# Layer 1 of a two-layer graph network: parts of 40, 40, 36 and 12 graphs instead of 40, 40, 40 and 8

## The chip, the cores and the metric

The kernel runs on one core of a Trainium2 chip. The metric is device time in microseconds (us) of one execution; lower is better. Times of "before" are the median of three runs. A profiled execution gives the trace; it has a time of its own, which stands beside its span below.

## The reference

There are 128 graphs of 128 nodes with 256 features each, all in float32. Two layers follow each other, both with a normalisation in front and a residual sum behind:

```
h = relu(layernorm(x));  x = x + L0(h, adj)
h = relu(layernorm(x));  x = x + L1(h, adj)

L0: conv 1x1 and conv of 17 taps with batch norms, a message product with
    A = exp(-dist) * adj, then a GRU cell over [conv, message] and h
L1: for each of 5 groups g of nodes (25, 9, 7, 6 and 6 nodes out of the first 25):
        A   = D^-1/2 (adj_g + I) D^-1/2
        hid = relu(A @ (h_g @ W1[g]) + b1[g])          # 256 -> 512
        out = relu(A @ (hid @ W2[g]) + b2[g])          # 512 -> 256
        fused[nodes of g] += softmax(fusion_w)[g] * out
```

Layer 1 touches only the first 25 nodes of a graph. The outputs are `out0` (the other 103 nodes, finished after layer 0) and `out1` (the 25 nodes, finished after layer 1).

## The kernel before

The graphs go in blocks of four (`BB`), so there are 32 blocks (`NBLK`). A front stage computes the convolution in the frequency domain and ends at about 470 us. Then comes the main loop over the blocks `i`: `gates(i, step, nxt)` issues the matmuls of the GRU cell (L666), and calls `step` between them. `step` hands out one piece of other work at a time. Turn by turn it takes either a piece of `first`, which is `beside_gates(i + 1)` and prepares the next block, or, on every second turn or when `first` is used up, a piece of layer 1. All these pieces are Python generators; each `yield` ends a piece. In the last block (`i == NBLK - 1`) a turn of layer 1 takes two pieces.

`beside_gates(i)` also contains `back(i - 2)`, the end of block `i - 2`: it adds the result to `xt`, copies the first 25 nodes to `xl` (L817), stores `out0` (L818), turns and normalises the 25 nodes (L830 to L839), multiplies them with the adjacency block `ae` (L843) and leaves the product in `ab` (L848). For the first three parts `xl` and `ab` go to scratch memory in DRAM (`xf`, L820, and `xa`, L853). For the last part (`LAST`) they stay on the chip, in `kept["f"]` and `kept["ax"]`.

Layer 1 works on parts of graphs, `PARTS`. `layer1(k)` is started when all blocks of part `k` have passed their gates: it is appended to `layer1s` after the gates of the block that follows the part, so part 2 of "before" comes after block 30's gates. It loads `f` (L959), waits for some turns, and goes over chunks. A chunk is a list of packs of at most 512 columns (a pack is a run of graphs of one group with at most 128 columns). For each group in a chunk, `first` multiplies with W1 (L934: 8 matmuls, as wide as the group's columns in the chunk), and ACT (L941) and DVE (L939) write `hh` in turn. Then each pack is multiplied with W2 (L994: 4 matmuls of 256 columns), ACT scales the result into `s2` (L997), and one pack later `last` multiplies it with the pack's adjacency tile `nt` (L913), ACT makes `og` (L916), and DVE adds it to `f` (L922). At the end `f` is stored to `out1` (L1008).

Three helpers issue loads while this goes on. `ax_load(n + 1)` loads the next chunk's `ax` (L905, tag "ax", two buffers). `prepare(j)` loads adjacency and degree tiles of pack `j + 5` (L864, L867) and lets DVE turn those of pack `j + 2` into `nt` (L871, L872). `weights1` and `weights2` load the weights of a later group (L881, each 512 KB) once the buffer of an earlier one is free: there are two buffers for W1 and three for W2. All these loads and stores are issued from one queue, SP's, in its order. A float32 matmul of the program appears as two records on PE in the trace.

Two buffers matter for the change. In "before" the last part's `kept["f"]` has the tag "f8", and `kept["ax"]` takes one of the two buffers of the tag "ax", for good, from the moment block 30's `back` runs.

After the loop the last block's end is written out by hand:

```python
end = back(NBLK - 1, *back_loads(NBLK - 1))
next(end)
for steps in (2, 1):
    next(end)
    for _ in range(steps):
        step()
for _ in end:
    pass
while layer1s:
    step()
for _ in layer1(LAST):
    pass
```

The program's instructions pass a scheduler that may move them on an engine; the order named in the text is the one that it made.

Of the kernel before, what the change touches and what calls it, by code (L numbers as in the profile page):

```python
# [8 lines left out]
F32 = mybir.dt.float32  # L9
# [4 lines left out]
P = 128  # L14
# [3 lines left out]
BB = 4  # L18
# [3 lines left out]
WCH = 32  # L22
STEP = 3
NR = LW - P
PARTS = [40, 40, 40, 8]
NN = 25
HID = 512
MW = 130
# [20 lines left out]
GW = GOFF[-1]  # L49
# [15 lines left out]

PACKS = [(k, p) for k, size in enumerate(PARTS) for c in _chunks(size) for p in c]

# [4 lines left out]
STOP = object()  # L72
# [3 lines left out]
def gnn_kernel(ctx: ExitStack, tc: tile.TileContext, io, out0: bass.AP, out1: bass.AP):  # L76
    nc = tc.nc
    x, adjT = io["x"], io["adjT"]
    NBLK, N, _, D = x.shape
    B, C = NBLK * BB, D // P  # L80
# [387 lines left out]
    l1 = ctx.enter_context(tc.tile_pool(name="l1", bufs=2, reuse_waits="tile"))  # L468
# [280 lines left out]
    def degrees(a, b, cs):  # L749
# [30 lines left out]
        for c0, c1, d in ((F0, K0, dvf), (K0, E0, dvk)):  # L780
# [5 lines left out]

    xa = [dram.tile([P, C, size * GW // BB], F32, tag=f"xa{k}", name=f"xa{k}") for k, size in enumerate(PARTS)]
    xf = [dram.tile([P, C, size, NN], F32, tag=f"xf{k}", name=f"xf{k}") for k, size in enumerate(PARTS)]
    first_of = [sum(PARTS[:k]) for k in range(len(PARTS) + 1)]
    where = [next((k, i * BB - first_of[k]) for k in range(len(PARTS)) if i * BB < first_of[k + 1])  # L790
             for i in range(NBLK)]
    LAST = len(PARTS) - 1
    kept = {}
# [9 lines left out]
    def back(i, ae, dc):  # L803

        xt, o = xts.pop(i), outs.pop(i)
        for c in range(C):
            nc.vector.tensor_add(xt[:, c, :], xt[:, c, :], o[:, c, :])
        xv = xt.rearrange("p c (b n) -> p c b n", b=BB)
        k, b0 = where[i]
        if k == LAST:  # L810
            if not kept:
                kept["f"] = l1.tile([P, C, PARTS[k], NN], F32, tag="f8", name="f8", bufs=2)
                kept["ax"] = l1.tile([P, C, 512], F32, tag="ax", name="ax", bufs=2)
            xl = kept["f"][:, :, b0:b0 + BB, :]
        else:
            xl = wk.tile([P, C, BB, NN], F32, tag="xl", name="xl", bufs=2)
        nc.vector.tensor_copy(xl, xv[:, :, :, :NN])  # L817
        nc.sync.dma_start(out0[i], xv[:, :, :, NN:])  # L818
        if k != LAST:
            nc.sync.dma_start(xf[k][:, :, b0:b0 + BB, :], xl)  # L820
        yield

        nc.vector.tensor_add(ae[:n4], ae[:n4], ie[:n4])
        for g in range(len(GROUPS)):
            av = ae[:n4, GOFF[g]:GOFF[g + 1]]
            nc.vector.tensor_scalar(av, av, dinv[:n4, E0 + 5 * i + g:E0 + 5 * i + g + 1], None, op0=ALU.mult)
        yield
        ps = bank()
        for c in range(C):
            nc.tensor.transpose(ps[:n4, c * P:(c + 1) * P], xl[:, c].rearrange("p b m -> p (b m)"), ident)  # L830
        st = l1.tile([P, 6], F32, tag="st", name="st", bufs=2)
        mv = l1.tile([P, 4], F32, tag="mv1", name="mv1", bufs=2)
        nc.vector.bn_stats(st[:n4], ps[:n4, :D])
        nc.vector.bn_aggr(mv[:n4, 0:2], st[:n4])
        nc.vector.tensor_scalar(mv[:n4, 2:3], mv[:n4, 1:2], EPS, None, op0=ALU.add)
        nc.gpsimd.tensor_tensor(mv[:n4, 3:4], mv[:n4, 2:3], mhalf[:n4, 0:1], op=ALU.pow)
        hn = l1.tile([P, D], F32, tag="hn", name="hn", bufs=1)
        nc.vector.tensor_scalar(hn[:n4], ps[:n4, :D], mv[:n4, 0:1], 0.0, op0=ALU.subtract, op1=ALU.max)
        nc.scalar.mul(hn[:n4], hn[:n4], mv[:n4, 3:4])  # L839
        yield  # L840
        ps = bank()
        for c in range(C):
            nc.tensor.matmul(ps[:, c * GW:(c + 1) * GW], hn[:n4, c * P:(c + 1) * P], ae[:n4], start=True, stop=True)  # L843
        if k == LAST:
            ab = kept["ax"][:, :, b0 // BB * GW:(b0 // BB + 1) * GW]
        else:
            ab = l1.tile([P, C, GW], F32, tag="ab", name="ab", bufs=1)
        nc.vector.tensor_tensor(ab, ps[:, :C * GW].rearrange("p (c m) -> p c m", c=C),  # L848
                                dc[:, None, :].to_broadcast([P, C, GW]), op=ALU.mult)
        if k != LAST:  # L850
            for g, (s, _) in enumerate(GROUPS):
                at = PARTS[k] * GOFF[g] // BB + b0 * s
                nc.sync.dma_start(xa[k][:, :, at:at + BB * s], ab[:, :, GOFF[g]:GOFF[g + 1]])  # L853
        yield
# [35 lines left out]
    def layer1(k):  # L890
        size, k5 = PARTS[k], len(GROUPS) * k
# [4 lines left out]
        for chunk in chunks:  # L896
            g, b0, _ = chunk[0]
# [56 lines left out]
        if k == LAST:  # L954
            f = kept["f"]
        else:
            tag = "f" if size > 8 else f"f{size}"
            f = l1.tile([P, C, size if size <= 8 else max(PARTS), NN], F32, tag=tag, name=tag, bufs=1 if size > 8 else 2)
            nc.sync.dma_start(f[:, :, :size, :], xf[k])  # L959
            yield  # L960
            for _ in range(8 if size > 8 else 2):
                yield
        for n, chunk in enumerate(chunks):
            ax_load(n + 1)
            hh = l1.tile([P, HID // P, 512], F32, tag="hh", name="hh", bufs=1)
            segs, done, at = [], {}, 0
            for g, b0, nb in chunk:
                m = nb * GROUPS[g][0]
                if not segs or segs[-1][0] != g:
                    segs.append((g, at, []))  # L970
                segs[-1][2].append((b0, nb, at, j))
                at += m
                done[g] = at if ends[g] == j else None
                j += 1
            bounds = [a for _, a, _ in segs] + [at]
            for t in range(len(segs) + 1):
                if t < len(segs):
                    g, m0, _ = segs[t]
                    m1 = bounds[t + 1]
                    if k == LAST:  # L980
                        xv = kept["ax"][:, :, :PARTS[k] // BB * GW].rearrange("p c (b m) -> p c b m", m=GW)
                        xv = xv[:, :, :, GOFF[g]:GOFF[g + 1]]
                    else:
                        xv = axs[n][:, :, m0:m1]
                    yield from first(g, m0, m1, xv)
                if t:
                    g, _, packs = segs[t - 1]
                    for b0, nb, at, jj in packs:
                        prepare(jj)
                        n1 = nb * GROUPS[g][0]  # L990
                        nt = ready.pop(jj)
                        ps = bank()
                        for q in range(HID // P):
                            nc.tensor.matmul(ps[:n1, :D], hh[:, q, at:at + n1], w2s[k5 + g][:, q, :],  # L994
                                             start=q == 0, stop=q == HID // P - 1)
                        s2 = l1.tile([P, D], F32, tag="s2", name="s2", bufs=3)
                        nc.scalar.mul(s2[:n1, :], ps[:n1, :D], dinv[:n1, K0 + jj:K0 + jj + 1])  # L997
                        if late:
                            last(*late.pop(0))
                        late.append((g, b0, nb, s2, nt))  # L1000
                        if jj == ends[g]:
                            weights2(k5 + g + 4)
                        yield
# [75 lines left out]
    layer1s = []  # L1079
    for i in range(NBLK):  # L1080
        first = beside_gates(i + 1) if i else second
        turn = [0]

        def step():

            next(degs, None)
            turn[0] += 1
            if (turn[0] % 2 if i else turn[0] % 3) and next(first, STOP) is not STOP:
                return
            for _ in range(2 if i == NBLK - 1 else 1):  # L1090
                while layer1s and next(layer1s[0], STOP) is STOP:
                    layer1s.pop(0)

        if i + 2 < NBLK:
            load_h(i + 2)
            load_y(i + 2)
        xts[i] = wk.tile([P, C, T], F32, tag="xt", name="xt", bufs=2)
        nc.sync.dma_start(xts[i], io["xT"][i])

        def nxt():  # L1100
            for _ in first:
                pass
            if i + 1 < NBLK:
                gate_inputs(i + 1, (0, 1))
            if i + 2 < NBLK:
                gate_inputs(i + 2, (2,))

        gates(i, step, nxt, None if i else sums_ahead)
        if (i + 2) * BB == PARTS[0]:
            for q in (-5, -4, -3):  # L1110
                prepare(q)
        for k in range(len(PARTS)):
            if i * BB == first_of[k + 1]:
                layer1s.append(layer1(k))

    end = back(NBLK - 1, *back_loads(NBLK - 1))
    next(end)
    for steps in (2, 1):
        next(end)
        for _ in range(steps):  # L1120
            step()
# [129 lines left out]
```

## Time and profile before

| what | value |
|---|---|
| median of 3 runs | 1843.83 us (1843.5 to 1846.31) |
| the profiled execution, its own time | 1844.07 us |
| its span in the trace | 1842.3 us |
| PE busy | 1825.6 us, 99% |
| DVE, ACT, POOL busy | 72%, 40%, 35% |
| W1 matmuls of layer 1 (L934) | 416 records |
| W2 matmuls of layer 1 (L994) | 480 records |
| last gate matmul of block 31 starts | 1792.40 us |
| last matmul of all starts (group of 8) | 1836.31 us |

PE is the matmul engine (TensorE), PEld its weight loads, DVE the vector engine, ACT the scalar engine, POOL GpSimd, SP the queue that issues transfers. L666 is line 666 of the kernel. A row such as "L994 PE MATMUL bank<-w,hh" names line, engine, operation, and output and inputs by the program's names. An arrow in square brackets gives the idle time in front of an instruction and what ended it. In the answers by windows each engine has its busy time in the stretch and its number of instructions; then come the clock granted to PE, the share of the DMA engines' time, and GB/s. Ends of matmuls are modelled, so spacings from start to start say more than durations.

### The profile page before, as it was taken

The numbers are of one execution on the slowest core, as the hardware profiler recorded it, in microseconds if no ns is written. First come the engines' busy times: TensorE is split into PE (matmuls) and PEld (weight loads), VectorE is DVE, ScalarE is ACT, GpSimd is POOL, SyncE is SP. The second block draws the span as 40 slices with busy tenths as digits, with TensorE's granted clock in tenths as the row PEclk, the third lists the DMA queues.
The fourth block names the chain that finished last, engine by engine and source line by source line (L and its number), as shares of the span: only waits on it lengthen the run. The fifth ranks groups of instructions, "written<-read, shape, count | busy, mean of one in ns | idle before, by whom it ended". The sixth has DMA issues, their size and how long they took to land.

```text
span 1842.3 us, 31240 instructions
## 1 busy us (share of the span) xinstructions
PE 1825.6 (99%) x10982; PEld 1591.2 (86%) x10982; DVE 1326.4 (72%) x3296; ACT 731.7 (40%) x1619; POOL 646.7 (35%) x803
## 2 busy tenths in 40 slices
PE   8999999999999999999999999999999999999998
PEld 6888888888888888888888888888888888888787
DVE  6888865555887878887665778778756677888543
ACT  4666641112434343334334333433343343333334
POOL 1111125675444443544221344435312243544200
PEclk9999999999999999999999999999999999999999
DMA  7888888996633333334324433333333433232125
GB/s 292 315 316 316 304 286 303 354 316 236 179 74 79 79 90 81 91 73 113 75 92 119 114 93 75 76 87 111 78 91 91 127 89 95 74 78 70 36 91 159
DMA packets 219420, 267.96 MB, mean 145 GB/s; under 512 B 106211, under 2 KB 182968, under 8 KB 217216
## 3 DMA queue, kind: packets, MB, share of 16 engines
q1 hardware_dynamic: 214079, 248.04, 44.9%
q10 hardware_dynamic: 5184, 17.93, 2.4%
q8 instruction: 87, 1.43, 0.3%
q14 instruction: 70, 0.57, 0.1%
HBM read 169.24 MB, written 96.67 MB: 144 GB/s over the span
## 4 chain that ended last, share of the span: by engine, by line
PE 94%; DVE 2%; DMA 2%; POOL 1%; SPq 0%; issue 0%; ACT 0%; ACTq 0%; DVEq 0%; POOLq 0%
PE bank L666 45%; PE bank L335 6%; PE bank L239 6%; PE bank L994 5%; PE bank L934 5%; PE bank L567 5%; PE bank L255 3%; PE bank L330 3%; PE bank L546 3%; PE bank L617 3%; PE bank L175 2%; PE bank L225 1%; PE bank L913 1%; PE bank L843 1%; DMA nt<-in_adjN_dram 1%; PE bank L528 1%
## 5 line engine op out<-in xcount | busy, mean ns | idle before, releaser
L666 PE MATMUL bank<-t,sw 128*128 128x256 f32 x1152 | 291.3, 380 | 0.6 <-DVE nn L681 0.3
L679 POOL TENSOR_TENSOR u<-u,m 128x256 f32<-128x256 f32 x128 | 95.4, 745 | 475.4 <-ACT m L677 404.5
L666 PEld LDWEIGHTS bank<-t,sw 128*128 128x128 f32 x1152 | 215.0, 190 | 32.3 <-issue 2.1
L666 PE MATMUL bank<-t,wih 128*128 128x256 f32 x768 | 200.3, 383 | 0.0
L666 PEld LDWEIGHTS bank<-t,wih 128*128 128x128 f32 x768 | 143.1, 190 | 28.8 <-DVE o L706 7.3
L239 PE MATMUL bank<-wc,ht 128*128 128x256 f32 x512 | 126.5, 392 | 0.0
L327 POOL TENSOR_TENSOR vs<-v 128x256 f32<-128x256 f32 x134 | 98.3, 759 | 71.3 <-DMA v<-vd 42.0
L994 PE MATMUL bank<-w,hh 128*125 128x256 f32 (+9 forms) x480 | 114.2, 380 | 1.0 <-DVE hh L939 1.0
L666 PE MATMUL bank<-xc,wih 128*128 128x256 f32 x384 | 114.6, 380 | 0.1
L666 PE MATMUL bank<-t,whh 128*128 128x256 f32 x384 | 114.5, 380 | 0.0
L666 PE MATMUL bank<-xn,wih 128*128 128x256 f32 x384 | 114.2, 379 | 0.0
L590 ACT ACTIVATE msg<-msg 128x512 f32<-128x512 f32 x64 | 36.8, 621 | 190.5 <-DVE msg L586 190.5
L666 PE MATMUL bank<-ht,whh 128*128 128x256 f32 x384 | 109.8, 380 | 0.0
L239 PEld LDWEIGHTS bank<-wc,ht 128*128 128x128 f32 x512 | 94.5, 194 | 15.0 <-issue 0.2
L934 PE MATMUL bank<-ax,w 128*128 128x500 f32 (+8 forms) x416 | 107.0, 396 | 0.0
L550 ACT ACTIVATE xc<-xc,bn 128x512 f32<-128x512 f32 x64 | 46.2, 722 | 151.1 <-DVE xc L549 151.0
L209 POOL TENSOR_TENSOR rs<-ve,mhalf 128x4 f32<-128x4 f32 x32 | 32.3, 1009 | 209.0 <-DVE ve L207 201.3
L994 PEld LDWEIGHTS bank<-w,hh 128*125 128x125 f32 (+9 forms) x480 | 84.1, 178 | 20.1 <-DVE hh L939 2.6
L184 ACT COPY sp<-bank 128x408 f32<-128x408 f32 (+1 forms) x160 | 66.8, 509 | 71.9 <-PE bank L175 68.9
L324 DVE SCALAR_TENSOR_TENSOR s<-X 128x256 f32<-128x256 f32 x67 | 46.7, 698 | 64.4 <-PE bank L335 64.4
L934 PEld LDWEIGHTS bank<-ax,w 128*128 128x128 f32 x416 | 69.8, 190 | 19.4 <-issue 12.3
L684 DVE TENSOR_TENSOR u<-bank,u 128x256 f32<-128x256 f32 x128 | 53.5, 418 | 42.9 <-PE bank L666 42.4
(206 smaller groups left out, 4363.8 us busy)
## 6 DMA issues: line engine op xcount, KB each, us to landing
vd<-sp SPq DMA_DIRECT2D x16, 2176.0 KB
v<-vd SPq DMA_DIRECT2D x34, 1024.0 KB
w<-in_w_dram SPq DMA_DIRECT2D x40, 512.0 KB
ln<-in_x_dram SPq DMA_DIRECT2D x32, 512.0 KB
htd<-ht SPq DMA_DIRECT2D x32, 512.0 KB
yd<-ys ACTq DMA_DIRECT2D x32, 512.0 KB
ht<-htd SPq DMA_DIRECT2D x32, 512.0 KB
ym<-yd SPq DMA_DIRECT2D x32, 512.0 KB
```

Source lines behind the costliest of these rows:

```text
L184: nc.scalar.copy(dst, s)
L239: nc.tensor.matmul(pv[:, bb, :], ht[:, c, b * N:(b + 1) * N], wc1[:, c, :], start=c == 0, stop=c == C - 1)
L255: nc.tensor.matmul(ps[:, bb * LW:(bb + 1) * LW], h1[:, 2 * h + bb, c * P:(c + 1) * P], fd, start=True, stop=True)
L327: nc.gpsimd.tensor_tensor(vs[:, c], vr[c], vi[c], op=ALU.add)
L330: nc.tensor.matmul(p1[:, :D], a[:, c], vs[:, c], start=c == 0, stop=c == C - 1)
L335: nc.tensor.matmul(ps[:, k * D:(k + 1) * D], u[:, c], w[c], start=c == 0, stop=c == C - 1)
L546: nc.tensor.matmul(ps[:, b * N:(b + 1) * N], ym[:, 2 * h + b, o * P:(o + 1) * P], idm, start=False, stop=b == 1)
L567: nc.tensor.matmul(ps[:, b, :], d[:, b * N:(b + 1) * N], w, start=True, stop=True)
L666: nc.tensor.matmul(ps, w, d, start=n == 0, stop=n == len(pairs) - 1)
L679: nc.gpsimd.tensor_tensor(got["u4"], got["u2"], got["m5"], op=ALU.add)
L934: nc.tensor.matmul(pv[:, q - q0, :], w1s[k5 + g][:, c, q * P:(q + 1) * P], xv[:, c], start=c == 0, stop=c == C - 1)
L994: nc.tensor.matmul(ps[:n1, :D], hh[:, q, at:at + n1], w2s[k5 + g][:, q, :], start=q == 0, stop=q == HID // P - 1)
```

## The change

The parts are 40, 40, 36 and 12 graphs. The last part so holds three blocks (29, 30 and 31) and the third nine, and `layer1(2)` is started after block 29's gates. The last part gets buffers of its own, "fl" for its features and "axl" for its products, each just as large as needed; the second "ax" buffer stays with `ax_load`. A turn of layer 1 takes one piece in every block. Beside the end of the last block six and two pieces are taken instead of two and one. The branches for a third part of eight graphs or fewer are gone. Lines after L954 move by one or two.

```diff
-PARTS = [40, 40, 40, 8]
+PARTS = [40, 40, 36, 12]
...
             if not kept:
-                kept["f"] = l1.tile([P, C, PARTS[k], NN], F32, tag="f8", name="f8", bufs=2)
-                kept["ax"] = l1.tile([P, C, 512], F32, tag="ax", name="ax", bufs=2)
+                kept["f"] = l1.tile([P, C, PARTS[k], NN], F32, tag="fl", name="fl", bufs=1)
+                kept["ax"] = l1.tile([P, C, PARTS[k] // BB * GW], F32, tag="axl", name="axl", bufs=1)
...
-            tag = "f" if size > 8 else f"f{size}"
-            f = l1.tile([P, C, size if size <= 8 else max(PARTS), NN], F32, tag=tag, name=tag, bufs=1 if size > 8 else 2)
+            f = l1.tile([P, C, max(PARTS), NN], F32, tag="f", name="f", bufs=1)
             nc.sync.dma_start(f[:, :, :size, :], xf[k])
             yield
-            for _ in range(8 if size > 8 else 2):
+            for _ in range(8):
                 yield
...
-                        xv = kept["ax"][:, :, :PARTS[k] // BB * GW].rearrange("p c (b m) -> p c b m", m=GW)
+                        xv = kept["ax"].rearrange("p c (b m) -> p c b m", m=GW)
...
-            for _ in range(2 if i == NBLK - 1 else 1):
-                while layer1s and next(layer1s[0], STOP) is STOP:
-                    layer1s.pop(0)
+            while layer1s and next(layer1s[0], STOP) is STOP:
+                layer1s.pop(0)
...
-    for steps in (2, 1):
+    for steps in (6, 2):
         next(end)
         for _ in range(steps):
             step()
```

The chunks of the parts follow from their sizes. Written as groups with their columns, a chunk in each bracket:

| part | chunks (columns of each group) |
|---|---|
| 40 graphs | (g0 500) (g0 500) (g1 360, g2 91) (g2 189, g3 240) (g4 240): 18 packs |
| 8 graphs | (g0 200, g1 72, g2 56, g3 48, g4 48): 6 packs |
| 36 graphs | (g0 450) (g0 450) (g1 324, g2 126) (g2 126, g3 216, g4 108) (g4 108): 17 packs |
| 12 graphs | (g0 300, g1 108, g2 84) (g3 72, g4 72): 7 packs |

## The prediction

> **What bounds the kernel now.** I read the page first: how busy each engine is, and which engine carries the chain that ended last.
>
> ```profile
> PE 1825.6 (99%) x10982; PEld 1591.2 (86%) x10982; DVE 1326.4 (72%) x3296; ACT 731.7 (40%) x1619; POOL 646.7 (35%) x803
> PEclk9999999999999999999999999999999999999999
> PE 94%; DVE 2%; DMA 2%; POOL 1%; SPq 0%; issue 0%; ACT 0%; ACTq 0%; DVEq 0%; POOLq 0%
> ```
>
> PE is busy 99% of 1842.3 us and is 94% of the chain; its clock stands at full speed. Time can therefore only come from PE work removed, from PE's idle time, or from the drain after its last matmul. Next, the windows: where PE is not full in the part of the span that the change touches.
>
> ```profile
> 1780.00:1790.00 10.00, 10.00 (x59) 9.01 (x58) 5.71 (x18) 5.31 (x13) 0.00 (x0) 1.00 0.18 59
> 1790.00:1800.00 10.00, 10.00 (x51) 8.54 (x50) 4.27 (x10) 3.76 (x8) 0.00 (x0) 1.00 0.63 170
> 1800.00:1810.00 10.00, 8.97 (x49) 7.48 (x48) 5.31 (x28) 4.68 (x11) 0.55 (x1) 1.00 0.87 178
> 1810.00:1820.00 10.00, 9.88 (x62) 9.00 (x61) 4.07 (x17) 4.04 (x11) 0.00 (x0) 1.00 0.55 182
> 1830.00:1843.00 13.00, 7.59 (x45) 5.37 (x44) 2.24 (x14) 4.05 (x11) 0.00 (x0) 0.92 0.06 18
> ```
>
> PE is full from 1400 to 1800, in the last two blocks too. It loses 1.03 us in 1800 to 1810, and the end is a drain. PE's timeline shows the place, DVE's the reason, and the list of waits (us in total, times, longest) that it happens nowhere else:
>
> ```profile
> 1806.59 0.59 PE L994 MATMUL bank<-w,hh 128*120 128x256 f32 x2
> 1807.44 1.12 PE L994 MATMUL bank<-w,hh 128*120 128x256 f32 x4 [0.25 <-DVE hh L939]
> 1809.34 0.69 PE L994 MATMUL bank<-w,hh 128*120 128x256 f32 x2 [0.78 <-DVE hh L939]
> ...
> 1804.98 0.26 DVE L871 TENSOR_TENSOR nt<-nt,ident 100x100 f32<-100x100 f32 x1 [3.10 <-DMA nt<-in_adjN_dram]
> ...
> PE bank L994 <- DVE hh L939: 1.0, 2, 0.8
> ```
>
> The second matmul of layer 1 waits for `hh`, because DVE sat 3.10 us at an adjacency tile not yet landed and then had a queue to work off. The ends of matmuls are modelled, so I take PE's cost from start to start. These eight records took 3.28 us (1806.59 to the next row, L843, at 1809.87); eight such elsewhere take 1.73 (1783.44 to 1785.16), 0.216 each. So 1.55 us are lost here, more than the 1.0 us that the waits of PE count, because a matmul is drawn past its end. From the last gate's end (1792.40 + 0.43) to the last matmul's (about 1837.4) 44.6 us pass for 41.5 us of such spacings: 3.1 us of waits, namely 1.55 here, 0.4 where L913 waits for `s` (1812.32 to 1813.59 for 0.86 of work), and 1.1 in gaps of 0.1 to 0.2 us after 1827. That is all that better timing could win.
>
> [...] eight L934 records of 56 columns take 0.86 us (1823.38 to 1824.24), 0.1075 each, and so do eight of 91 (1773.89 to 1774.75); a narrower matmul costs no less. [...] a weight load issued at 1790.11 moved data until about 1793.5, 3.4 us, and I use that. [...] `out0` has 412 B pieces, and in 1800 to 1804, with it in flight, the core moved 93 to 260 GB/s where weight loads alone moved 330 to 390.
>
> **The change, part by part.**
>
> *Matmul widths (L934).* Each group of a chunk gives 16 records, at 0.00084 us a column (500 wide: 1747.95 to 1751.30 for eight, 0.419 each) and at least 0.1075. Before, third part (500, 500, 360, 91, 189, 240, 240): 16 x 1.813 = 29.0; last part (200, 72, 56, 48, 48): 16 x 0.598 = 9.6. After, 36 graphs (450, 450, 324, 126, 126, 216, 108, 108): 16 x 1.64 = 26.2; 12 graphs (300, 108, 84, 72, 72): 16 x 0.682 = 10.9. From 38.6 to 37.1: **-1.4 us**, all on PE. The columns are equal in sum; fewer lie under the floor.
>
> *Packs (L994, L913).* 18+18+18+6 = 60 before, 18+18+17+7 = 60 after; eight and four records each, at 0.216 and 0.108 whatever the pack holds. Zero. `prepare` issues one adjacency and one degree load per pack: 60 each as before.
>
> *Block 29 in the last part.* Three blocks, not two, leave `xl` and `ab` on chip: six small stores (L820, five of L853) fewer on SP. PE never waited for them: zero.
>
> *Steps dealt out.* Layer 1's third part is appended after block 29's gates, not 30's, and takes one step per turn beside two blocks instead of two per turn beside one; beside the last `back` it takes 6+2 steps, not 2+1. The same matmuls move on PE, which is full in both places. In the earlier parts the same mix of one step per turn beside a full block ran without a PE wait at `hh` (both waits of the list lie in the tail), so DVE (76% busy in 1000 to 1400) covers it: zero. SP issues the third part's loads earlier, with slack of over 10 us to their use.
>
> *Own buffers.* `axl` and `fl` free the second `ax` buffer. The wait that this removes was at SP (L905 waited 4.5 us for PE L994, with adjacency loads queued behind it), not at PE. What it delayed is the 3.10 us of DVE and so the **1.55 us** at `hh`. In the changed order of PE the last `back` (L830, L843) lies between other matmuls, and the last chunk is one pack of 108 columns: I let the 1.55 go.
>
> *What is late next.* Behind the last gate now stand 48.7 us of spacings, not 41.5, and two W1 buffers rotate over narrower groups. W1 of group 4 takes group 2's buffer: it is issued once the second half of group 2 (126 wide) has run and is needed after sixteen records of 216 columns (2.9 us) and one pack (1.7): 4.6 us later. SP issues it right behind `out0` of block 30 (412 KB). With 3.4 us alone it just fits. Behind `out0` it may take as long as the 512 KB load at 1798.10 did, which by its bytes was through at about 1804.5: 6.4 us. So PE waits 0 to 2.2 us; I take 0.7. Behind that load stand the next W1, and the three adjacency tiles that DVE must have before `hn` and `hh`; PE's L843 and the last L994 wait for those: 0 to 2 us, and less the longer W1 has already held PE up; I take 0.4. L913 directly after the last L994 now has no other L913 before it: it waits for all of `s` (0.2 + 0.47 + about 0.15), 0.8 not 0.4: **+0.4**. Together **+1.5**, from +0.4 to +4.
>
> *The drain.* `fl` is 300 KB against 200, in 1200 B pieces against 800. [...] **+0.25**.
>
> *Sum.* -1.4 - 1.55 + 1.5 + 0.25 = **-1.2 us**. Against the profiled execution (span 1842.3, time 1844.07) this gives 1842.9; that execution lies 0.24 above the median 1843.83, so against the median **1842.6**. A difference under 0.2% (3.7 us) is about what a measurement of this kernel can tell from none, so this counts as no change.
>
> **The rivals.**
>
> *No wait is left in the tail.* W1 arrives in time and the small gaps after 1827 vanish with the narrow groups: -1.4 - 3.1 + 0.8 (L913 must wait) + 0.25 gives -3.5, about 1840.3; only with the 0.8 hidden too does it pass 3.7. For it: the 48-wide groups, where the small gaps lie, are gone. Against: the last part has more transitions, and W1 with its 4.6 us against 3.4.
>
> *W1 of group 4 comes late, and the tail ends slower than before.* With 2.2 us there, 2 us more at L843 and `hh` behind the adjacency tiles, and 0.4 at L913: -1.4 - 1.55 + 4.6 + 0.25 = +1.9, about 1845.7. It decides from the point where W1 and the tiles together hold PE up for over 2.3 us; to be slower by 0.2% they would need 6 us. For it: the measured 6.4 us behind `out0`. Against: every us that PE waits is a us of slack for all the loads after it.
>
> *The change does not do what it says:* the steps are dealt evenly but to places where PE was full anyhow, and DVE is still late at `hh`. Then 1.55 stays: 1844.1.
>
> **How the numbers follow.** Forecast (-2.5 to +0.5) 0.6; no wait left 0.12; slower by W1 0.18; `hh` still late 0.1. Of the fast case a third passes 3.7 us, and 0.04 is for a gain I don't see: faster 0.08. Of the slow case a third could pass it if more loads fall behind in turn, and 0.04 for waits elsewhere: slower 0.1. The rest, 0.82, is no change. The range takes in both outer cases: 1840.2 to 1845.8.
>
> **What would show it.** L934's busy starts fall by 1.4 us, with forms of 450, 324, 216 and 108 columns and none of 48; L994 keeps 480 records. No PE wait for DVE `hh` of over 0.5 us; a PE wait for DMA `w` at L934 some 9 us after the last gate (or none, with W1 in time); block 31's gates with PE full. Wrong would be: PE idle in the blocks of 30 and 31, a tail with over 5 us of waits, or L934's sum unchanged.

## The result, and the profile after

The changed kernel takes 1847.8 us in the median of 16 runs (1844.95 to 1850.79), the kernel before 1843.15 in 16 runs beside it (1841.41 to 1846.31). The ratio is 1.0020, with a 95% interval of 1.0012 to 1.0027: some 3.7 us slower, where 1.2 us of gain were forecast. A repetition of the same kernel (below) gave 1.0019. The profiled execution took 1848.56 us, with a span of 1846.8.

From the page of the changed kernel, the busy line, the chain's shares and the row of L934 among the costliest groups (busy us, mean ns of one, then idle time in front of it and what ended most of it):

```profile
PE 1825.1 (99%) x10998; PEld 1590.5 (86%) x10998; DVE 1328.0 (72%) x3296; ACT 731.6 (40%) x1621; POOL 648.0 (35%) x803
PE 92%; DVE 2%; DMA 2%; POOL 1%; SPq 1%; issue 1%; ACT 0%; ACTq 0%; DVEq 0%; POOLq 0%
L934 PE MATMUL bank<-ax,w 128*128 128x500 f32 (+9 forms) x352 | 94.5, 404 | 2.5 <-DMA w<-in_w_dram 2.5
```

PE's busy time is 0.5 us lower, its span 4.5 us longer, so the time went into PE's idle time. Where, the list of PE's waits of the changed kernel says (us in total, times, longest):

```profile
PE bank L934 <- DMA w<-in_w_dram: 2.5, 1, 2.5
PE bank L666 <- ACT xc L550: 1.5, 1, 1.5
...
PE bank L605 <- DVE lr L598: 0.9, 3, 0.3
PE bank L913 <- ACT s L996: 0.8, 2, 0.6
PE bank L666 <- POOL t L641: 0.6, 3, 0.2
```

The wait for `hh` that stood in this list before is gone. In its place is W1, with 2.5 us, and there are more small waits for POOL's `t` and DVE's `lr` (three each, where "before" has one each), which belong to the preparation of a block. The 1.5 us for `xc` lie ahead of 560 us, at the first blocks, which the change does not touch. PE's timeline of the changed kernel, its end:

```profile
1795.75 1.89 PE L993 MATMUL bank<-w,hh 128*126 128x256 f32 x8
1800.15 1.14 PE L934 MATMUL bank<-ax,w 128*128 128x108 f32 x8 [2.51 <-DMA w<-in_w_dram]
1811.90 1.89 PE L993 MATMUL bank<-w,hh 128*108 128x256 f32 x8
1814.36 0.69 PE L913 MATMUL bank<-nt,s 108*128 108x108 f32 x4 [0.56 <-ACT s L996]
1841.10 0.67 PE L913 MATMUL bank<-nt,s 72*128 72x72 f32 x4 [0.22 <-ACT s L996]
```

The 108 wide row is group 4, whose W1 the prediction called in danger. From start to start, 1795.75 to 1800.15 is 4.40 us for eight records worth 1.73: 2.67 us lost.

**By stage.** Two executions of the same code differ by up to 3 us in the first 1660 us (front stage, starts of the first parts), so spans must not be compared whole. I cut the trace at the first edge matmul (L523) of blocks 30 and 31, at the last gate (L666) and at the start of the last four matmuls (L913 of the last pack; in "before" the group of eight at 1836.31 holds two packs, and the last four start at 1837.00). Us:

| kernel | block 30 to 31 | to the last gate | to the last matmul | to the end | sum |
|---|---|---|---|---|---|
| before | 36.12 | 95.08 | 44.60 | 5.30 | 181.1 |
| after | 37.76 | 86.81 | 53.11 | 5.70 | 183.4 |

Block 30 begins at 1661.2 before and at 1663.4 after; these 2.2 us of the 4.5 lie ahead of everything that the change moves, and the repetition has them not (1660.4). The other 2.3 us are the change's. The first column shows a loss that the prediction did not have at all: +1.64 us between blocks 30 and 31, where 36.12 us is what a block without a new part takes.

DVE's timeline of the changed kernel in that stretch:

```profile
1669.89 0.41 DVE L684 TENSOR_TENSOR u<-bank,u 128x256 f32<-128x256 f32 x1
1673.70 0.46 DVE L871 TENSOR_TENSOR nt<-nt,ident 125x125 f32<-125x125 f32 x2 [3.40 <-DMA nt<-in_adjN_dram]
1674.08 0.41 DVE L687 TENSOR_TENSOR nn<-u,bank 128x256 f32<-128x256 f32 x1
```

And that of the kernel before, one block later:

```profile
1708.00 0.29 DVE L871 TENSOR_TENSOR nt<-nt,ident 125x125 f32<-125x125 f32 x1 [4.47 <-DMA nt<-in_adjN_dram]
```

It is the same instruction: the sum of the third part's first adjacency tile with the identity. DVE reaches it before the tile has landed and stands still, with all that is queued behind. In "before" this falls at the end of block 30's gates (1678.27 to 1714.17, by the count of gate matmuls, 126 a block). Behind it come block 31's gates, beside which no further block is prepared. In "after" the part is ready a block earlier: the wait falls at the end of block 29's gates (to 1680.27), and behind it stand the inputs of block 30's gates and the preparation of block 31. What that does, in the changed kernel's timelines of POOL and then PE:

```profile
1678.48 0.72 POOL L679 TENSOR_TENSOR u<-u,m 128x256 f32<-128x256 f32 x1 [7.37 <-DVE u L674]
```

```profile
1685.69 1.13 PE L666 MATMUL bank<-t,sw 128*128 128x256 f32 x4 [0.24 <-POOL t L641]
1693.98 0.44 PE L605 MATMUL bank<-ident,lr 128*128 128x128 f32 x2 [0.31 <-DVE lr L598]
```

POOL stood 7.37 us for DVE's `u`, so its `t` came late, and PE's list shows the short waits for it. Each is drawn as 0.2 to 0.3 us only; the interval between the blocks shows the whole 1.64. In "before" POOL stood even longer at this place, and PE did not wait behind it:

```profile
1712.96 0.73 POOL L679 TENSOR_TENSOR u<-u,m 128x256 f32<-128x256 f32 x1 [8.61 <-DVE u L674]
```

There POOL then has four instructions on `t` to do (1714.33 to 1717.84), in "after" eight (1679.85 to 1687.91), since another block is to be prepared.

### The profile page after: what moved, and what is told of

Read it like the earlier page. It is cut to its first block, busy times and chain, and to the rows that moved or that the text cites. A ratio compares the mean times of both kernels' runs of the same rounds, so it can differ in the third digit from the quotient of the medians.

```text
span 1846.8 us, 31270 instructions
## 1 busy us (share of the span) xinstructions
PE 1825.1 (99%) x10998; PEld 1590.5 (86%) x10998; DVE 1328.0 (72%) x3296; ACT 731.6 (40%) x1621; POOL 648.0 (35%) x803
## 4 chain that ended last, share of the span: by engine, by line
PE 92%; DVE 2%; DMA 2%; POOL 1%; SPq 1%; issue 1%; ACT 0%; ACTq 0%; DVEq 0%; POOLq 0%
PE bank L666 44%; PE bank L335 6%; PE bank L239 6%; PE bank L993 5%; PE bank L934 5%; PE bank L567 5%; PE bank L255 3%; PE bank L330 3%; PE bank L617 3%; PE bank L546 3%; PE bank L175 2%; PE bank L225 1%; PE bank L913 1%; PE bank L843 1%; DMA nt<-in_adjN_dram 1%; PE bank L523 1%
## 5 line engine op out<-in xcount | busy, mean ns | idle before, releaser
L666 PE MATMUL bank<-t,sw 128*128 128x256 f32 x1152 | 292.0, 380 | 0.9 <-POOL t L641 0.6
L666 PEld LDWEIGHTS bank<-t,sw 128*128 128x128 f32 x1152 | 214.6, 190 | 33.9 <-issue 3.0
L666 PE MATMUL bank<-t,wih 128*128 128x256 f32 x768 | 200.2, 383 | 0.0
L666 PEld LDWEIGHTS bank<-t,wih 128*128 128x128 f32 x768 | 143.2, 190 | 29.3 <-DVE o L706 6.3
L666 PE MATMUL bank<-xc,wih 128*128 128x256 f32 x384 | 114.9, 381 | 1.5 <-ACT xc L550 1.5
L666 PE MATMUL bank<-t,whh 128*128 128x256 f32 x384 | 114.5, 380 | 0.0
L666 PE MATMUL bank<-xn,wih 128*128 128x256 f32 x384 | 114.2, 379 | 0.0
L993 PE MATMUL bank<-w,hh 128*125 128x256 f32 (+9 forms) x480 | 113.6, 380 | 0.1
L666 PE MATMUL bank<-ht,whh 128*128 128x256 f32 x384 | 110.0, 380 | 0.0
L993 PEld LDWEIGHTS bank<-w,hh 128*125 128x125 f32 (+9 forms) x480 | 84.4, 178 | 18.1 <-DVE hh L939 1.2
L934 PE MATMUL bank<-ax,w 128*128 128x500 f32 (+9 forms) x352 | 94.5, 404 | 2.5 <-DMA w<-in_w_dram 2.5
L332 ACT COPY k<-bank 128x256 f32<-128x256 f32 x67 | 24.9, 372 | 146.7 <-PE bank L330 144.1
```

Source lines behind the costliest of these rows:

```text
L666: nc.tensor.matmul(ps, w, d, start=n == 0, stop=n == len(pairs) - 1)
L934: nc.tensor.matmul(pv[:, q - q0, :], w1s[k5 + g][:, c, q * P:(q + 1) * P], xv[:, c], start=c == 0, stop=c == C - 1)
```

## The experiments

**The theory** after this reading has two parts. (1) W1 of group 4 meets the last block's `out0` store and arrives 2.2 to 2.7 us late. (2) The third part's first adjacency tile holds DVE up ahead of block 31's preparation, 1.64 us. **Rivals**: the difference is scatter between runs; W1 lacks a buffer, and `out0` has nothing to do with it; the third part's generator simply starts too early; the sizes of the parts are to blame.

All ratios are to the kernel before, with 95% intervals; every kernel was run beside it on the same chip.

**The changed kernel again** (no edit).

> The changed kernel itself, again, beside before. Theory A (two loads come late: W1 of group 4 behind the last out0 store, 2.7 us, and the first adjacency tiles of part 3 in front of block 31's preparation, 1.6 us; less 1.4 of narrow matmuls and the 1.55 wait at hh): both waits stand again at their places, and the time is 2 to 5 us above before. Theory B (the loss comes from somewhere in the first 1660 us, where the traces already differ by 2.2 us): the shift at the last gates but two differs from run to run and the two waits do not repeat.

Ratio 1.0019 (1.0011 to 1.0026), so the loss is no scatter. Stages: 37.90, 86.81, 54.24, 5.67, sum 184.6. PE's wait for W1 was shorter, 2.22 us, and yet its tail is 1.1 us longer. The windows of this run (busy us and count for PE, PEld, DVE, ACT, POOL, then the granted clock, DMA share, GB/s) say why:

```profile
1796.00:1798.00 2.00, 1.04 (x8) 1.04 (x9) 0.00 (x0) 0.00 (x0) 0.00 (x0) 0.94 0.97 285
1798.00:1800.00 2.00, 2.00 (x11) 1.99 (x11) 0.69 (x3) 1.13 (x3) 0.00 (x0) 0.50 0.93 301
1800.00:1802.00 2.00, 2.00 (x12) 1.83 (x10) 1.62 (x11) 0.70 (x3) 0.55 (x1) 0.70 0.04 10
```

After the idle time the clock was halved for about 3.4 us ((0.06 + 0.50 + 0.30) x 2 us, over 0.5). In the first profile of the changed kernel it was not:

```profile
1800.00:1802.00 2.00, 1.85 (x16) 1.85 (x17) 0.29 (x1) 0.56 (x2) 0.00 (x0) 1.00 1.00 331
```

So the wait can cost about 1.4 us more than its own length (54.24 - 53.11, and 0.3 for the shorter wait). The granted clocks on record suggest that it does so in about half of the executions: the clock of the whole execution was 0.996 or less in 17 of the 32 executions of the changed kernel here and above, but in 4 of 60 of the kernel before beside this run and in none of 13 of the next run.

**The last `out0` held back** until the last part's first pack, the order on PE being kept. A data dependence holds the store (an element of it is written with 0 x `s2` + itself).

```diff
-        nc.sync.dma_start(out0[i], xv[:, :, :, NN:])
+        if i != NBLK - 1:
+            nc.sync.dma_start(out0[i], xv[:, :, :, NN:])
+        else:
+            kept["out"] = xv
...
+                        if jj == NPK - 7:
+                            one = kept["out"][:n1, 0, 0, NN:NN + 1]
+                            nc.vector.scalar_tensor_tensor(one, s2[:n1, 0:1], 0.0, one, op0=ALU.mult, op1=ALU.add)
+                            nc.sync.dma_start(out0[NBLK - 1], kept["out"][:, :, :, NN:])
```

> The changed kernel, with the out0 store of the last block held back until the first pack of the last part, so that W1 of group 4 has nothing in front of it; the order of PE is the same. Theory A: the load takes about 3.4 us after its issue, PE's wait of 2.5 us at L934 falls to under 0.3, and the time is 2 to 3 us under e1_again. Rival A2 (the load is slow by itself or for the adjacency tiles, the store only stands beside it): PE still waits 1.5 us or more, the time moves under 1 us. Theory B: no change in time.

Ratio 1.0002 (0.9994 to 1.0010). No wait for `w` remains in PE's list, and the third stage falls to 50.33 us, from 53.11 and, with the half clock, 54.24; the first, 37.84, stays. Part (1) of the theory holds, and it alone takes the kernel back to the time of before.

**A third W1 buffer**, with W1 asked for one group earlier.

```diff
-        weights(w1s, "w1", 2, [P, C, HID], upto)
+        weights(w1s, "w1", 3, [P, C, HID], upto)
...
-                    weights1(k5 + g + 3)
+                    weights1(k5 + g + 4)
...
-            weights1(2)
+            weights1(3)
```

> The changed kernel with three W1 buffers instead of two, so that W1 of group 4 is issued a group earlier, while out0 stays where it is. Theory A: no PE wait for a W load in the tail, 2 to 3 us under e1_again, like e2. Rival A2: the same here, so e2 is the run that tells it. Theory B: no change.

Ratio 1.0009 (1.0002 to 1.0015). W1 is in time, but DVE, and after it PE, now wait for the next thing on SP's queue. DVE's timeline and PE's waits of this kernel:

```profile
1801.73 0.26 DVE L871 TENSOR_TENSOR nt<-nt,ident 100x100 f32<-100x100 f32 x1 [1.70 <-DMA nt<-in_adjN_dram]
```

```profile
PE bank L843 <- ACT hn L839: 1.8, 1, 1.8
```

The adjacency tiles, and with them `hn` and L843, are what is "late next", as the prediction said of them; the stage is 53.82 us, no better than with the W1 wait, since the clock was halved here too (0.65 and 0.50 in the windows of 2 us from 1804 to 1808). But this execution (1848.96 us) lies 3.2 above the median of its runs, and only 2 of the 21 had a granted clock of 0.996 or less. By the ratios the buffer takes back about half of the loss, though the intervals overlap.

**L871 left out** (the tile is then used without the identity's sum), first in the changed kernel, then in the kernel before.

```diff
-            ops = [nc.vector.tensor_add(nt[:n, :n], nt[:n, :n], ident[:n, :n]),
-                   nc.vector.tensor_mul(nt[:n, :n], nt[:n, :n], dc[:n, :n])]
-            tc.keep_in_program_order(ops[1])
+            ops = [nc.vector.tensor_mul(nt[:n, :n], nt[:n, :n], dc[:n, :n])]
+            tc.keep_in_program_order(ops[0])
```

> The changed kernel without L871, the sum of the adjacency tile and the identity (the self loops in the second product of layer 1 are left out): DVE then has no early instruction that waits for the adjacency tiles, only L872, which keeps its place. 120 DVE instructions' worth of 60 x 0.28 us go, all beside PE. Theory A: no DVE wait at the start of the three parts, block 31's preparation takes 36.1 us between its edge-term matmuls instead of 37.8, and the parts 1 and 2 lose their 1 us too: 1.5 to 3.5 us under e1_again. Rival (POOL is slow there by itself[...]): the block stays at 37 us or more.

> The kernel before, without L871 as in e4 (the self loops of layer 1's second product are left out). It tells which share of e4's gain belongs to the change. Theory A: only the starts of parts 1 and 2 are freed (about 3 us together, which both kernels pay), part 3's start costs the kernel before nothing because no block is prepared any more beside its last block's gates; the tail's wait at hh goes too, since the tile that held DVE there is one of L871's: 3 to 4.5 us under before. Rival (L871's load on DVE as such slows the kernel in every block): the gain spreads over the blocks without layer 1 too.

Changed kernel: ratio 0.9991 (0.9984 to 0.9998); the interval between blocks 30 and 31 is 36.12 us, exactly that of before, while the wait for W1 (2.17 us) and the half clock after it stay (weight loads of these matmuls took up to 338 ns in this profile, 192 at most in the first of the changed kernel). The multiplication L872 stays where the program puts it; it was only L871 that the scheduler had moved up, to where its tile could at the earliest be there. Kernel before: ratio 0.9976 (0.9966 to 0.9985), but from other places: its stages from block 30 on sum to 180.3 (181.1 before), with 95.07 us to the last gate as before, so the third part's wait cost nothing there; and 4.2 us come off between blocks 2 and 22, where parts 1 and 2 start and pay the same wait in both kernels. Its blocks without layer 1 stay at 36.12. So part (2) holds: the wait is old, and what the change did was to put a third one where it costs something.

**Own buffers alone**, in the kernel before.

```diff
-                kept["f"] = l1.tile([P, C, PARTS[k], NN], F32, tag="f8", name="f8", bufs=2)
-                kept["ax"] = l1.tile([P, C, 512], F32, tag="ax", name="ax", bufs=2)
+                kept["f"] = l1.tile([P, C, PARTS[k], NN], F32, tag="fl", name="fl", bufs=1)
+                kept["ax"] = l1.tile([P, C, 512], F32, tag="axl", name="axl", bufs=1)
```

> The kernel before, with the last part's own buffers alone; parts and steps as before. Theory A: SP is no longer held by L905, DVE's 3.1 us at the adjacency tile and PE's 1.55 us at hh shrink, 0 to 1.5 us under before. Rival (the tile is late because of the out0 store and the weight loads in front of it, not because of L905): DVE and PE wait as before, no change.

Ratio 1.0003 (0.9996 to 1.0009): not to be told from none. The trace shows the effect: the wait for `hh` is gone, and from the last gate to the last matmuls it takes 43.08 us for 44.60, which is the predicted 1.5. It drowns in the scatter ahead of block 30 (this profile has 1.9 us more between blocks 2 and 22).

**The third part started one block later**, with two pieces a turn in the last block, as in "before".

```diff
-            while layer1s and next(layer1s[0], STOP) is STOP:
-                layer1s.pop(0)
+            for _ in range(2 if i == NBLK - 1 else 1):
+                while layer1s and next(layer1s[0], STOP) is STOP:
+                    layer1s.pop(0)
...
-            if i * BB == first_of[k + 1]:
+            if i * BB == first_of[k + 1] + (BB if k == LAST - 1 else 0):
```

> The changed kernel with part 3 started one block later, where the kernel before starts it, and two steps a turn in the last block; parts 40, 40, 36, 12, own buffers and the end's 6+2 steps stay. Theory A: the block between the last two edge-term matmuls takes 36.1 us instead of 37.9; W1 of group 4 gets gate matmuls between release and use; but the end of the last block stands bare (L843 right behind L830), 2 to 2.5 us of wait. Net 0 to 3 us under e1_again. Rival (the early start costs nothing, the 1.8 us come from the last part's third block): the block still takes 37.8 us.

A miss: ratio 1.0036 (1.0024 to 1.0049), and the interval is 38.23 us, not 36.1. DVE's timeline has the wait at its old place:

```profile
1673.41 0.49 DVE L871 TENSOR_TENSOR nt<-nt,ident 125x125 f32<-125x125 f32 x2 [4.51 <-DMA nt<-in_adjN_dram]
```

The generator's start does not set where L871 stands. SP stores the products of the part's last block (L853), and right behind them it loads `ax` (L905) and then the tiles (L864): at 1663.87, 1667.79 and 1668.40 here, at 1664.60, 1668.52 and 1669.13 in "after". L871 stands where this first tile is on its way. It is the sizes of the parts that fix after which block this is, as the next run confirms. On top, the adjacency tiles came late in the tail (2.5 us at L843), and with that wait the clock stood at half for 10.2 us (below full by 0.37, four times 0.50 and 0.19 in the windows of 2 us from 1812 to 1824). This execution, 1853.34 us, lies 3.3 above the median of its runs.

**The old sizes, all else changed**: parts of 40, 40, 40 and 8.

```diff
-PARTS = [40, 40, 36, 12]
+PARTS = [40, 40, 40, 8]
```

> The changed kernel with the old parts 40, 40, 40, 8; own buffers and the new dealing of steps stay. e7 did not tell the start apart: its trace has DVE's wait at the same place, since the scheduler puts loads and L871 where the part's last block is ready, not where the generator starts. Theory A (the part's end one block earlier puts the adjacency tiles in front of block 31's preparation; narrow groups leave W1 no time): the last block interval is 36.1 us again, no PE wait for W1 (11 us from release to use), about 2.5 to 4 us under e1_again, near the kernel before. Rival (the new dealing of steps costs the time): as slow as e1_again.

Ratio 1.0010 (1.0001 to 1.0019). The interval is back at 36.12, DVE's wait of 4.47 us is one block later again (at 1707.62), and there is no wait for `w`. But the end of block 30 now waits 1.66 us at L843 for `hn` (1727.69), a wait that "before" does not have. The sum from block 30 on is 182.3 us. Both losses of the changed kernel thus come with the new sizes. The new dealing of steps is not free either: with the old sizes and the buffers alone, the sum was 179.7, 2.6 us less. The ratios, 1.0010 and 1.0003, differ by less, and their intervals overlap.

**Adjacency tiles issued from ACT's queue**, in the kernel before, in the changed one, and in the changed one with `out0` held back.

```diff
-            ins = nc.sync.dma_start(nt[:n, :n], io["adjN"][j + 5, :n, :n])
+            ins = nc.scalar.dma_start(nt[:n, :n], io["adjN"][j + 5, :n, :n])
```

> The kernel before with the adjacency loads from ACT's queue as in e8. Theory A: the starts of parts 1 and 2 are freed (about 3 us, as in e5) and the wait at hh shrinks: 2 to 4.5 us under before. Whether the parts of 36 and 12 are worth anything once the waits are gone is then e8 against this run: by the widths 1.4 us less, by the longer bare tail up to 1 us more. Rival (the tiles gain nothing from the other queue, e8's gain was the store's): no change.

> The changed kernel with the adjacency loads from ACT's queue alone; out0 stays in front of W1. Theory A: block interval 36.1 us, the W1 wait of 2 to 2.7 us remains, with or without a fall of the clock behind it: 3.5 to 5 us under e1_again and 2.5 to 4 us over e8. Rival (W1 is late because of the adjacency tiles in front of and behind it in the queue, not for the store): the W1 wait goes too, and the time is that of e8.

> The changed kernel with out0 of the last block held back as in e2, and the adjacency tiles of L864 issued from ACT's queue instead of SP's, where they do not stand behind ax, f and weight loads. Nothing is left out. Theory A: DVE's waits at L871 fall to under 1 us, the starts of all parts are free, W1 is in time: 4 to 7 us under e1_again, so 1.5 to 3.5 under before. Rival (the DMA engines are the limit there, not the queue): the tiles land no earlier, and the time is that of e2.

| kernel | ratio (95%) | block 30 to 31 | to the last gate | to the last matmul | to the end | sum |
|---|---|---|---|---|---|---|
| before, tiles on ACT | 0.9988 (0.9980 to 0.9997) | 36.12 | 95.07 | 44.17 | 5.25 | 180.6 |
| after, tiles on ACT | 1.0011 (1.0005 to 1.0018) | 36.16 | 86.85 | 55.69 | 5.70 | 184.4 |
| after, tiles on ACT, `out0` held | 0.9975 (0.9968 to 0.9983) | 36.17 | 86.86 | 50.69 | 5.68 | 179.4 |

With the tiles on ACT's queue, the loss ahead of block 31 is gone without a change in the computation. All three kernels also gain at the starts of parts 1 and 2: 791.7 us from block 2 to block 22, where "before" takes 795.1. In the middle row W1 is later than ever (issued at 1789.50, 7.4 us ahead of its use), so by the ratios this kernel gains 1.5 us on the repetition, not the 3.5 to 5 expected; PE's timeline:

```profile
1796.94 1.84 PE L934 MATMUL bank<-ax,w 128*128 128x108 f32 x8 [3.67 <-DMA w<-in_w_dram]
```

and with the half clock after it (0.80, 0.50 and 0.85 in the windows of 2 us from 1796 to 1802) that stage takes 5.0 us more than with `out0` held. The last row, with a median of 1838.69 us, beats both kernels. Against the first row it is 1.2 us shorter in the stages and about 0.1% by the ratios, whose intervals just overlap. Not all of this is the change's: the first row still has a wait of 0.8 us for `hh`, and holding `out0` back was not tried there.

**The last `out0` from ACT's queue**, to see whether W1 is late for its place in SP's queue or for the company.

```diff
-        nc.sync.dma_start(out0[i], xv[:, :, :, NN:])
+        (nc.scalar if i == NBLK - 1 else nc.sync).dma_start(out0[i], xv[:, :, :, NN:])
```

> The changed kernel, with one edit: the last block's out0 store is issued from ACT's queue instead of SP's, at about the same time; SP's queue then has W1 of group 4 with nothing in front of it, while the 412 KB of out0 are still moved at about the same time. What it tells apart: theory A, W1 is late because it stands behind out0 in SP's queue: then the two share the DMA engines from the moment W1 is issued, W1 takes 4 to 5.5 us from issue to use instead of 6.9, and PE waits 0 to 0.8 us at L934; the time falls 1 to 3 us against the changed kernel (2.0 to 2.5 us of wait gone, no half clock), ratio to before about 1.0005. Theory B, the engines have so much to do with out0's small pieces that any load beside it takes as long, from whichever queue: then the PE wait for w stays at 2 to 2.7 us and the ratio stays at 1.0019. Under both the block interval in front of block 31 stays at 37.8 us, since its adjacency loads are not touched, and ACT loses under 0.2 us for the issue.

Ratio 1.0027 (1.0016 to 1.0039): nothing gained; the stages are 37.65, 86.80, 54.30 and 5.7, sum 184.5. Timelines of this kernel's ACT queue, SP queue and PE, and its DMA queues from 1785 to 1806 us (packets, MB, share of 16 engines):

```profile
1791.02 0.63 ACTq L818 DMA_DIRECT2D out_dram<-xt  x1
```

```profile
1791.77 3.31 SPq L881 DMA_DIRECT2D w<-in_w_dram  x2
```

```profile
1798.68 1.59 PE L934 MATMUL bank<-ax,w 128*128 128x108 f32 x8 [2.29 <-DMA w<-in_w_dram]
```

```profile
q1 hardware_dynamic: 2050, 2.26, 41.1%
q10 hardware_dynamic: 1040, 0.42, 14.9%
```

From issue to use W1 takes 6.9 us, as behind `out0` in SP's queue (1793.24 to 1800.15 in "after"). Theory B of this run holds: it is not the order of a queue. The packets of the store, 1040 for 0.42 MB, take 14.9% of 21 us of all 16 engines, 3.1 us, with W1 under way beside them: the DMA share was 1.04, 1.24 and 1.04 in the windows of 2 us from 1792 to 1798. Whether the size of the pieces, 412 B, counts in it no run here tells. The 3.1 us are a time in company: block 29's store, with no other transfer beside it in "after" (1690 to 1696), took 35.1% of 6 us, 2.1 us. So the 6.9 us of W1 are more than the store alone and a load alone (2.1 + 3.4) together. Two more weight loads and three adjacency tiles went out while W1 was under way; what each of them adds no run here tells.

## Why the prediction was wrong, and where it was right

**Where the sum failed.**

- *What is late next, the W1 term.* The mechanism and the place were named; the term was mis-sized: 0 to 2.2 us, 0.7 taken, 2.67 measured, and 2.2 to 2.5 as PE's wait in all four profiles in which `out0` went out beside this load and the tiles came from SP. The prediction had the better number in hand, 6.4 us for a 512 KB load behind `out0`, and took a value between it and the 3.4 of an undisturbed load. The measured time is 6.9. (The store is block 31's, not block 30's as the text has it.) Its rival "W1 of group 4 comes late" was the closest to the result.
- *Steps dealt out: zero.* This step failed outright. It looked for a PE wait at layer 1's own matmuls and took DVE's mean load as cover. What moved, with the sizes, was a DVE wait on a DMA, 3.4 to 4.5 us long, from a block behind which nothing more is prepared to one behind which a block is: 1.64 us (1.5 to 1.8 in the runs with the start as changed). The trace of before showed the wait, at 1708.00, and at the starts of parts 1 and 2; the text says of SP's loads that they have "slack of over 10 us to their use", which does not hold for L871.
- *The clock.* The text takes full speed. After the wait the clock was at half for about 3.4 us in three of the four profiles with `out0` beside W1 on the computation as changed (the repetition, tiles on ACT, `out0` on ACT; 0.50 in one window of 2 us of each, 0.70 to 0.94 in the windows next to it): some 1.4 us, as the repetition shows it, that no step has.
- *"All that better timing could win"*, 3.1 us in the tail. This was too little: the starts of parts 1 and 2 cost both kernels some 4 us, as the runs without L871 show, though the list of PE's waits hardly names them.

**Where it held.**

- *Own buffers*: -1.55 forecast; with the buffers alone in "before" the stage fell by 1.5, and in "after" no wait for `hh` is left.
- *Widths*: L934 has 352 + 80 = 432 records for 416, in the forms expected, and L994 (now L993) none more. Summed from start to start over all its records, L934 takes 97.19 us before and 95.84 after: -1.35, where -1.4 was forecast.
- *L913 must wait*: 0.8 forecast; 0.73 measured from start to start, 1811.90 to 1814.36 less 1.73, for 0.41 before.
- *L843 and `hh` behind the adjacency tiles*: 0.4 taken, none seen in "after", 1.8 with W1 in time and `out0` still beside the tiles (third W1 buffer). The rival added this to the full W1 wait; the runs show one in the place of the other.
- *The drain*: +0.25 forecast, as the author's estimate; at the 330 to 390 GB/s that weight loads moved in the trace of before, 100 KB more are an estimate of 0.26 to 0.31. From the last four matmuls on +0.4 was measured. Of this 0.3 lies from the issue of the last store to the end (1838.74 to 1842.3 before, 1842.92 to 1846.8 after).

**The sum again**, from block 30 on. Laid over the records behind the last gate, the prediction's spacings give 41.2 us of work before and 48.3 after (it had 41.5 and 48.7), so the waits there are 3.4 and 4.8 us: +1.4, where -1.55 + 1.5 was forecast. With -1.4 for the widths (by the same spacings), +0.4 for the drain and +1.64 ahead of block 31 this gives +2.0, where the stages show +2.3; 0.3 us I can't assign to a step. With the half clock it is +3.5 in the repetition (184.6 for 181.1). The ratio's +3.7 (2.2 to 5.0) lies there too.

## What to carry to other kernels

When work starts earlier, look for the first instruction of it that waits for a transfer, on whichever engine, and ask what will then be queued behind it; a wait that costs nothing at the end of a program can cost something a block earlier (1.64 us here). When a load goes out beside a store, take the time that such a load took in company from the trace (6.4 us here, not 3.4), even if another queue issues the store (6.9 us from either queue here). Moving the store out of the way gained more than a further buffer, which in part handed the wait to the next transfer (1.0002 against 1.0009, with intervals that overlap). Compare stages between fixed landmarks, since spans of the same code differed by more than the effect.

## What the runs showed of the hardware that was not expected

After one idle stretch of PE the clock was halved in six profiles: after 1.76 us (third W1 buffer), 2.17 (L871 left out), 2.22 (the repetition), 2.29 (`out0` on ACT), 2.52 (third part started later) and 3.67 us (tiles on ACT). It was not after 2.51 us in the first profile of the changed kernel, nor after 1.66 with the old sizes. It stood at half for 3.4 us in the repetition, and again with a third W1 buffer (0.35 and 0.50 below full in two windows of 2 us); but with the third part started later it was 10.2 us, with a further idle stretch of 0.69 us within. With the third W1 buffer it set in only after PE had started again: PE resumes at 1803.28, the window of 1802 to 1804 is still at full clock, and the next at 0.65. What decides between these cases no run here shows.
